# Attention scores in two-bank PSUM tiles, and the products of two groups of heads in one bank

## The chip, the cores and the metric

The kernel runs on one core of a Trainium2 chip. A core has five engines that work in parallel, each through its own instructions in order: TensorE (PE) multiplies matrices, VectorE (DVE) and ScalarE (ACT) work on elements, GpSimd (POOL) and SyncE (SP) do the rest, mostly issuing DMA transfers. PE writes its results to PSUM, which has 2 KB banks on each of 128 partitions: a bank holds 512 float32 values a partition. The metric is the device time of one execution in microseconds (us). Times of the kernel before are the median of three runs, and beside them there is one profiled execution, whose records are read below.

## The reference

One transformer layer over x of shape (8, 512, 128) in float32: eight sequences (B) of 512 tokens (T) with 128 features (D). Causal attention with 16 heads of 8 features comes first, then a mixture of 8 experts of which every token uses its best two. Cut to what matters:

```python
def attn(x):                       # after a layernorm of x
    q = (x @ Wq).reshape(b, t, 16, 8); k, v likewise
    s = einsum('bqhd,bkhd->bhqk', q * 8 ** -0.5, k)
    s = where(causal, s, -inf)
    p = softmax(s)                 # exp(s - max), divided by its sum over keys
    o = einsum('bhqk,bkhd->bqhd', p, v).reshape(b, t, 128)
    return o @ Wo + bo
x = x + attn(layernorm(x))
def moe(x):                        # after a layernorm of x
    probs = softmax(x @ gate_w.T); top2 = top_k(probs, 2)
    out_e = relu(x @ w1[e] + b1[e]) @ w2[e] + b2[e]
    return sum over the token's two experts of prob * out_e
x = x + moe(layernorm(x))
```

## The kernel before

A sequence's 512 tokens are cut into four blocks of 128 (`NT` = 4), and its 16 heads into four groups of four (`G`, `HG`); a group is two pairs of heads. Everything for one pair (sequence b, group g) is done in turn, 32 such groups in all.

**Scores, twice.** `shifts` (lines 555 to 636) computes the scores s = q k^T only to find each row's maximum: PE writes a bank of 512 scores (lines 593 and 598, bf16 operands that hold float32 split into three parts and the causal mask as extra rows), and DVE reduces it to maxima `pm` (line 612). The negated maxima of the group (`nm`, line 618) are turned by PE (line 560), copied by ACT to `nmT` (line 562) and sent by DMA as two more rows of q (line 568). `attend` (lines 638 to 760) then computes the transposed scores st (lines 740 and 745), which now come out with the maximum already subtracted, and ACT takes their exponential into `pt` (line 750), one bank at a time. The products of `pt` with v (line 667) add up in the one PSUM bank `po`: four heads lie in four strips of 32 partitions, of which each uses 9, eight features and a row of sums (v is kept with a column of ones in `va`). After a group's last product ACT copies the bank to `ob` (line 675); `divide` turns it by four PE transposes (`oqp`, line 687), takes the reciprocals of the sums (line 690) and scales (line 691). After the last group of a sequence `out_T` and `out_project` apply Wo.

**Units.** The causal scores of a pair of heads are laid into banks by `S_UNITS` and `T_UNITS` (lines 83 to 92): five banks of 512 columns for each pair and each of the two kinds, as two units of two banks and one unit of a single bank. So a group has ten banks of scores, ten maxima, ten banks of transposed scores and ten exponentials. All these banks come from one pool, `ps_sc`, with four buffers of a bank each (line 123), taken in turn by both kinds; after attention, expert tiles take their hidden layer `ph` (line 1238) from it as well. `ps_mm` has three more banks, and `po` has the eighth.

**Order.** Each engine's order is fixed by the program. Generators such as `project`, `shifts`, `attend`, `route` and `experts` yield virtual times, in units of one sequence, and the one that is due first goes on. `shifts` runs 0.55 ahead of `attend` (`LEAD`), and a unit of scores and a unit of transposed scores come in turn: PE's order is scores, transposed scores, some product, other work, scores again. After each unit of scores one entry of the list `late` is run (maxima turned, then their DMA on SP's queue); after each unit of transposed scores `go_on` runs one waiting product and one waiting step of the output. Layernorms, projections, routing and, from the fourth sequence on, expert tiles lie between these units on every engine.

Of the kernel before, what the change touches and what calls it, by code (L numbers as in the profile page):

```python
# [18 lines left out]
P = 128  # L19
# [7 lines left out]
def preln_attn_moe(ctx: ExitStack, tc: tile.TileContext, x, wq, wk, wv, wo, bo,  # L27
# [54 lines left out]

    S_UNITS = (
        (((0, 3, 0),), ((1, 3, 0),)),
        (((0, 0, 0), (0, 2, P)), ((1, 0, 0), (1, 2, P))),
        (((0, 1, 0), (1, 1, 2 * P)),),
    )
    T_UNITS = (
        (((0, 0, 0),), ((1, 0, 0),)),
        (((0, 1, 0), (0, 3, 3 * P)), ((1, 1, 0), (1, 3, 3 * P))),  # L90
        (((0, 2, 0), (1, 2, 2 * P)),),
    )

# [29 lines left out]
    ps_sc = ctx.enter_context(tc.tile_pool(name="ps_sc", bufs=4, space=PSUM))  # L123
# [106 lines left out]
    def packed_buffers(k):  # L230
        q2 = const.tile([P, H, T], BF16, tag=f"q2{k}", name=f"q2{k}")
        k2 = const.tile([P, H, T], BF16, tag=f"k2{k}", name=f"k2{k}")
        q2_buf.append(q2)
        k2_buf.append(k2)
        va = const.tile([P, NT, H, VC], F32, tag=f"va{k}", name=f"va{k}")
        nc.gpsimd.memset(va[:, :, :, HD:], 1.0)
        va_buf.append(va)
        pm = const.tile([P, HG, 4, 4], F32, tag=f"pm{k}", name=f"pm{k}")
        nc.gpsimd.memset(pm, NEG)
        pm_buf.append(pm)  # L240
        nh = const.tile([P, P], BF16, tag=f"nh{k}", name=f"nh{k}")
        nc.gpsimd.memset(nh, 0.0)
        nh_buf.append(nh)
# [149 lines left out]
    def project():  # L393
# [4 lines left out]
        def arrange(k, groups):  # L398
            for s, w in enumerate((wq_sb, wk_sb)):
                t = const.tile([P, D], F32, tag=f"w{k}{s}", name=f"w_{k}_{s}")  # L400
                nc.scalar.copy(
                    t.rearrange("k (g d h) -> k g d h", g=groups, d=HD),
                    w.rearrange("k (g h d) -> k g d h", g=groups, d=HD),
                )
# [150 lines left out]
    def shifts():  # L555
# [18 lines left out]
        for b in range(B):  # L574
            for g in range(G):
# [5 lines left out]
                pm = pm_buf[g % 2].rearrange("p (n u) t k -> p u n (t k)", u=2)  # L581
                for pr in range(2):
                    n = 2 * g + pr
                    for i, unit in enumerate(S_UNITS):
                        yield t0 + (3 * pr + i) / 24
                        for v, bank in enumerate(unit):
                            ps = ps_sc.tile(
                                [P, T], F32, tag="sc", name=f"s_{b}_{n}_{i}_{v}"
                            )
                            for u, t, at in bank:  # L590
                                h, q = 2 * n + u, ts(t, P)
                                if t > 0:
                                    nc.tensor.matmul(  # L593
                                        ps[:, at : at + t * P], lhsT=q2[:KS, h, q],
                                        rhs=k2[:KS, h, : t * P],
                                        start=(at == 0), stop=True, skip_group_check=True,
                                    )
                                nc.tensor.matmul(  # L598
                                    ps[:, at + t * P : at + (t + 1) * P],
                                    lhsT=q2[:, h, q], rhs=k2[:, h, q],  # L600
                                    start=(at + t == 0), stop=True, skip_group_check=True,
                                )
                            blocks = ps.rearrange("p (a q) -> p a q", q=P)
                            if i == 0:
                                top, src = pm[:, v, pr, 12:13], ps
                            elif i == 1:
                                top, src = pm[:, v, pr, 3:7], blocks
                            else:
                                top, src = pm[:, :, pr, 8], ps.rearrange(
                                    "p (u k) -> p u k", u=2  # L610
                                )
                            nc.vector.tensor_reduce(top, src, AX.X, ALU.max)  # L612
                        if t0 + (3 * pr + i) / 24 < 0:
                            keep_warm(WARM[2], f"{g}_{pr}_{i}")
                        if late:
                            late.pop(0)()
# [21 lines left out]
    def attend():  # L638
# [14 lines left out]
        def at_cols(pt, unit, u, at, W):  # L653
            v = u if len(unit) == 2 else 0
            return pt[:, v, at : at + W]

        def product(b, g, pts, unit, first, last):
            va = va_buf[b % 2]
            for j in sorted({j for bank in unit for _, j, _ in bank}):
                W = T - j * P  # L660
                for pr in range(2):
                    for bank in unit:
                        for u, i, at in bank:
                            if i != j:
                                continue
                            h = 2 * pr + u
                            nc.tensor.matmul(  # L667
                                po[32 * h : 32 * h + VC, j * P :],
                                lhsT=va[:, j, HG * g + h, :],
                                rhs=at_cols(pts[pr], unit, u, at, W),  # L670
                                start=(first and j == 0), stop=(last and j == 2),
                            )
            if last:
# [8 lines left out]
        def divide(b, ob, g):  # L682
            if g == 0:
                on[b] = work.tile([P, NT, D], F32, tag="on", name=f"on_{b}", bufs=1)
            pt = mm_tile(f"oqp_{b}_{g}")
            for t in range(NT):
                nc.tensor.transpose(pt[:, ts(t, P)], ob[:, ts(t, P)], ident)  # L687
            oq = pt.rearrange("p (k r) -> p k r", r=32)
            rd = small.tile([P, NT * HG], F32, tag="rd", name=f"rd_{b}_{g}")
            nc.vector.reciprocal(rd, oq[:, :, HD])  # L690
            nc.vector.tensor_tensor(
                on[b].rearrange("p t (g h d) -> p t g h d", g=G, h=HG)[:, :, g],
                pt.rearrange("p (t h r) -> p t h r", t=NT, h=HG)[:, :, :, 0:HD],
                rd.rearrange("p (t h) -> p t h", t=NT).unsqueeze(3).to_broadcast(
                    [P, NT, HG, HD]
                ),
                ALU.mult,
            )
# [22 lines left out]
        for b in range(B):  # L721
            for g in range(G):
                yield b + g / G
                assert (b, g, 2) in shifted
                q2, k2 = q2_buf[b % 2], k2_buf[b % 2]
                for i, unit in enumerate(T_UNITS):
                    pts = []
                    for pr in range(2):
                        yield b + g / G + (2 * i + pr + 0.5) / 24
                        n = 2 * g + pr  # L730
                        pt = work.tile(
                            [P, 2, T], F32, tag="pt", name=f"pt_{b}_{n}_{i}", bufs=6
                        )
                        for v, bank in enumerate(unit):
                            ps = ps_sc.tile(
                                [P, T], F32, tag="sc", name=f"st_{b}_{n}_{i}_{v}"
                            )
                            for u, j, at in bank:
                                h, k = 2 * n + u, ts(j, P)
# [294 lines left out]
    def experts():  # L1034
# [17 lines left out]
        def after(s, i):  # L1052
            return when(s, quad(s, i)[0]) >= B
# [321 lines left out]
```

## Time and profile before

| | |
|---|---|
| median of three runs | 618.14 us (616.91 to 624.91) |
| the profiled execution | 610.58 us, of which its span 608.9 us |
| mean granted clock of PE | 0.949 |
| PE busy | 526.4 us, 86% |
| DVE busy | 435.1 us, 71% |
| ACT busy | 312.2 us, 51% |
| POOL busy | 188.4 us, 31% |
| maxima of scores (DVE, line 612) | 320, 208 us together, from 25.4 to 448 us |
| exponentials (ACT, line 750) | 320, 177.6 us, from 44.4 to 485 us |
| products with v (PE, line 667) | 1,024, 99.5 us |
| copies of po (ACT, line 675) | 32, 18.9 us |

The span runs from the first to the last instruction of the program. Busy times are those of the instructions' records; a matmul's end is modelled, and matmuls overlap, so a busy PE is not PE at its peak. A row such as "L612 DVE TENSOR_REDUCE pm<-s ... x320 | 206.4, 683 | 31.2" names the line, the engine, the operation and its tiles, the number of instructions, their busy time in us and the mean ns of one, and last the time for which the engine stood idle just before them and what ended that. The chain of work that ended last is followed back from the last instruction: at each step to what released it, or to the instruction before it on its engine.

### The profile page before, as it was taken

The numbers are of one execution on the slowest core, as the hardware profiler recorded it, in microseconds if no ns is written. First come the engines' busy times: TensorE is split into PE (matmuls) and PEld (weight loads), VectorE is DVE, ScalarE is ACT, GpSimd is POOL, SyncE is SP. The second block draws the span as 40 slices with busy tenths as digits, with TensorE's granted clock in tenths as the row PEclk, the third lists the DMA queues.
The fourth block names the chain that finished last, engine by engine and source line by source line (L and its number), as shares of the span: only waits on it lengthen the run. The fifth ranks groups of instructions, "written<-read, shape, count | busy, mean of one in ns | idle before, by whom it ended". The sixth has DMA issues, their size and how long they took to land.

```text
span 608.9 us, 14141 instructions
## 1 busy us (share of the span) xinstructions
PE 526.4 (86%) x4804; PEld 381.0 (63%) x4804; DVE 435.1 (71%) x1407; ACT 312.2 (51%) x685; POOL 188.4 (31%) x220
## 2 busy tenths in 40 slices
PE   7879998988877888889899999998999889889980
PEld 4655455555444554656566677775667579789970
DVE  6787688678986777787888786898684256323594
ACT  2646566655564574546455565564464434244530
POOL 3032200203413230162243213514314534655441
PEclk9989799999987899999899999999899999899995
DMA  2658187286379436521662486232135588667793
GB/s 56 177 135 169 44 215 164 67 186 169 80 152 166 116 96 166 135 60 44 156 145 60 119 173 170 71 87 88 49 81 145 163 252 234 181 196 240 218 315 111
DMA packets 68762, 86.07 MB, mean 141 GB/s; under 512 B 11540, under 2 KB 50748, under 8 KB 66652
## 3 DMA queue, kind: packets, MB, share of 16 engines
q1 hardware_dynamic: 63300, 75.10, 49.0%
q0 software_dynamic: 4800, 9.41, 4.6%
q8 instruction: 39, 0.64, 0.5%
q10 hardware_dynamic: 592, 0.66, 0.3%
q14 instruction: 31, 0.25, 0.2%
HBM read 61.34 MB, written 26.16 MB: 144 GB/s over the span
## 4 chain that ended last, share of the span: by engine, by line
PE 48%; DVE 24%; ACT 9%; DMA 7%; issue 7%; SPq 2%; another core or an unknown queue 1%; POOL 1%; ACTq 0%; DVEq 0%; POOLq 0%
DVE pm L612 11%; PE po L667 10%; PE py L1097 7%; PE ph L1238 6%; ACT pt L750 5%; PE st L745 4%; PE s L593 4%; PE st L740 4%; PE s L598 3%; PE oqp L687 3%; DMA q<-nmT 2%; DMA q<-ys 2%; PE pq L444 2%; DVE x L1316 2%; ACT hT L1245 2%
## 5 line engine op out<-in xcount | busy, mean ns | idle before, releaser
L750 ACT ACTIVATE pt<-st 128x512 f32<-128x512 f32 x320 | 177.6, 599 | 133.3 <-PE st L740 55.5
L612 DVE TENSOR_REDUCE pm<-s 128x1 f32<-128x512 f32 (+2 forms) x320 | 206.4, 683 | 31.2 <-PE s L598 25.7
L1135 POOL DMA_INDIRECT ys<-yo,to x78 | 75.5, 968 | 139.3 <-ACT pt L750 21.6
L593 PE MATMUL s<-k,q 72*128 72x384 bf16 (+2 forms) x384 | 94.6, 282 | 19.5 <-DVE pm L612 9.2
L740 PE MATMUL st<-q,k 128*128 128x128 bf16 x512 | 94.0, 225 | 12.6 <-DMA q<-nmT 4.6
L598 PE MATMUL s<-k,q 128*128 128x128 bf16 x512 | 94.9, 225 | 7.3 <-ACT pt L750 4.9
L667 PE MATMUL po<-pt,va 128*9 128x512 f32 (+3 forms) x1024 | 99.5, 460 | 1.1 <-ACT pt L750 1.0
L1003 POOL DMA_INDIRECT xs<-xn_f,slot x64 | 62.2, 972 | 116.8 <-ACT pt L750 85.1
L745 PE MATMUL st<-q,k 74*128 74x256 bf16 (+2 forms) x384 | 94.6, 284 | 0.0
L1097 PE MATMUL py<-w_sb,hT 128*128 x624 | 87.1, 281 | 7.7 <-issue 4.5
L1097 PEld LDWEIGHTS py<-w_sb,hT 128*128 128x128 f32 x624 | 77.7, 194 | 10.0 <-issue 5.5
L598 PEld LDWEIGHTS <-q 128*128 128x128 bf16 x512 | 51.6, 101 | 30.9 <-issue 27.8
L593 PEld LDWEIGHTS <-q 72*128 72x128 bf16 x384 | 38.2, 101 | 37.7 <-issue 31.3
L740 PEld LDWEIGHTS <-k 128*128 128x128 bf16 x512 | 52.5, 103 | 12.1 <-issue 5.2
L745 PEld LDWEIGHTS <-k 74*128 74x128 bf16 x384 | 38.4, 100 | 19.6 <-issue 14.3
L667 PEld LDWEIGHTS po<-pt,va 128*9 128x9 f32 x1024 | 21.3, 90 | 35.5 <-issue 24.0
L1238 PE MATMUL ph<-xgT,wt 128*128 128x128 f32 x288 | 40.1, 282 | 0.7 <-ACT xgT L1199 0.6
L1238 PEld LDWEIGHTS ph<-xgT,wt 128*128 128x128 f32 x288 | 35.0, 192 | 5.4 <-PE st L740 1.7
L1245 ACT ACTIVATE hT<-ph,q 128x128 f32<-128x128 f32 x72 | 20.9, 371 | 27.9 <-PE ph L1238 14.8
L690 DVE RECIPROCAL rd<-oqp 128x16 f32<-128x16 f32 x32 | 8.2, 255 | 36.9 <-PE oqp L687 31.6
L687 PEld LDWEIGHTS oqp<-ident,ob 128*128 128x128 f32 x128 | 14.4, 148 | 29.7 <-issue 28.3
L454 POOL TENSOR_TENSOR part<-rest,part 128x512 bf16<-128x512 f32 x14 | 16.1, 1158 | 50.0 <-ACT part L453 21.8
(170 smaller groups left out, 717.2 us busy)
## 6 DMA issues: line engine op xcount, KB each, us to landing
wt<-wrows SPq DMA_DIRECT2D x36, 322.0 KB
k<-kparts SPq DMA_DIRECT2D x42, 192.0 KB
q<-wrows SPq DMA_DIRECT2D x24, 322.0 KB
k<-wrows SPq DMA_DIRECT2D x18, 322.0 KB
q<-qparts SPq DMA_DIRECT2D x30, 192.0 KB
q<-ys SPq DMA_DIRECT2D x15, 256.0 KB
k<-xs SPq DMA_DIRECT2D x42, 65.0 KB
qparts<-part SPq DMA_DIRECT2D x14, 192.0 KB
```

Of the source, the lines that this page charges most:

```text
L593: nc.tensor.matmul(ps[:, at : at + t * P], lhsT=q2[:KS, h, q], rhs=k2[:KS, h, : t * P], start=(at == 0), stop=True, skip_group_check=True,)
L598: nc.tensor.matmul(ps[:, at + t * P : at + (t + 1) * P], lhsT=q2[:, h, q], rhs=k2[:, h, q], start=(at + t == 0), stop=True, skip_group_che ...
L612: nc.vector.tensor_reduce(top, src, AX.X, ALU.max)
L667: nc.tensor.matmul(po[32 * h : 32 * h + VC, j * P :], lhsT=va[:, j, HG * g + h, :], rhs=at_cols(pts[pr], unit, u, at, W), start=(first and ...
L740: nc.tensor.matmul(ps[:, at : at + P], lhsT=k2[:, h, k], rhs=q2[:, h, k], start=(at == 0), stop=True, skip_group_check=True,)
L745: nc.tensor.matmul(ps[:, at + P : at + T - j * P], lhsT=k2[:KO, h, k], rhs=q2[:KO, h, (j + 1) * P :], start=False, stop=True, skip_group_c ...
L750: last_exp[0] = nc.scalar.activation(pt[:, v, :], ps, AF.Exp, scale=SCALE)
L1003: ins = nc.gpsimd.indirect_dma_start(out=xs[k], out_offset=bass.IndirectOffsetOnAxis(ap=slot[b][:, j * NT + i : j * NT + i + 1], axis=0), ...
L1097: nc.tensor.matmul(py, lhsT=hT[:, c, :], rhs=w2_sb[:, bass.ds(at[s, i] + c * E * D, D)], start=(c == 0), stop=(c == FC - 1),)
L1135: ins = nc.gpsimd.indirect_dma_start(out=ys[k], out_offset=bass.IndirectOffsetOnAxis(ap=to[s, first][:, i - first : i - first + 1], axis=0 ...
L1238: nc.tensor.matmul(ph[:, ts(c, P)], lhsT=wt[s, i][:, ts(c, P)], rhs=turned[s, first][:, ts(i - first, P)], start=True, stop=True,)
L1245: nc.scalar.activation(hT[:, c, :], ph[:, ts(c, P)], AF.Relu, bias=bias)
```

## The change

It has two parts. First, every unit is two banks, and a tile of `ps_sc` is two banks too, with two buffers instead of four: a group has five units of each kind, each reduced by one maximum instruction or one exponential of 1,024 elements a partition. The single-bank units of a group's two pairs are joined to one. Products are put off to the second, fourth and fifth unit of a group. Second, `va` has 18 columns a head, nine of v and sums and nine of zeros, and the heads are put in another order by the arrangement of Wq's and Wk's columns, so that the products of an even group go to rows 0 to 8 of each strip of `po` and those of the next, odd group to rows 9 to 17 of the same strip: `po` is copied, turned and divided once for two groups. The tiles of the experts' hidden layer take the two halves of a two-bank tile in turn.

```diff
     S_UNITS = (
-        (((0, 3, 0),), ((1, 3, 0),)),
-        (((0, 0, 0), (0, 2, P)), ((1, 0, 0), (1, 2, P))),
-        (((0, 1, 0), (1, 1, 2 * P)),),
+        (((0, 0, 3, 0),), ((0, 1, 3, 0),)),
+        (((0, 0, 0, 0), (0, 0, 2, P)), ((0, 1, 0, 0), (0, 1, 2, P))),
+        (((1, 0, 3, 0),), ((1, 1, 3, 0),)),
+        (((1, 0, 0, 0), (1, 0, 2, P)), ((1, 1, 0, 0), (1, 1, 2, P))),
+        (((0, 0, 1, 0), (0, 1, 1, 2 * P)), ((1, 0, 1, 0), (1, 1, 1, 2 * P))),
     )
...
-    ps_sc = ctx.enter_context(tc.tile_pool(name="ps_sc", bufs=4, space=PSUM))
+    ps_sc = ctx.enter_context(tc.tile_pool(name="ps_sc", bufs=2, space=PSUM))
...
-        va = const.tile([P, NT, H, VC], F32, tag=f"va{k}", name=f"va{k}")
-        nc.gpsimd.memset(va[:, :, :, HD:], 1.0)
+        va = const.tile([P, NT, H, 2 * VC], F32, tag=f"va{k}", name=f"va{k}")
+        nc.gpsimd.memset(va[:, :, :, HD : HD + 1], 1.0)
+        nc.gpsimd.memset(va[:, :, :, VC:], 0.0)
...
-                nc.scalar.copy(
-                    t.rearrange("k (g d h) -> k g d h", g=groups, d=HD),
-                    w.rearrange("k (g h d) -> k g d h", g=groups, d=HD),
-                )
+                for p in range(2):
+                    src = w[:, ts(p, 64)].rearrange("k (h o d) -> k o d h", o=2, d=HD)
+                    of = "k (d o h) -> k o d h" if groups == 2 else "k (o d h) -> k o d h"
+                    nc.scalar.copy(t[:, ts(p, 64)].rearrange(of, o=2, d=HD), src)
...
+                for i, unit in enumerate(S_UNITS):
+                    yield t0 + i / (UNITS * G)
+                    ps = ps_sc.tile([P, 2, T], F32, tag="sc", name=f"s_{b}_{g}_{i}")
+                    for v, bank in enumerate(unit):
+                        for pr, u, t, at in bank:
+                            ...
+                    nc.vector.tensor_reduce(top, src, AX.X, ALU.max)
...
+        def product(b, g, pts, first, last):
+            odd = g % 2
+            va = va_buf[b % 2].rearrange("p c h r -> p c (h r)")
+            ...
+            for j, h, p in sorted(parts, key=lambda a: a[:2]):
+                c0 = 2 * VC * (8 * (g // 2) + 2 * h + odd) - VC * odd
+                nc.tensor.matmul(
+                    po[32 * h : 32 * h + 2 * VC, j * P :], lhsT=va[:, j, c0 : c0 + 2 * VC], rhs=p,
+                    start=(first and j == 0 and not odd), stop=(last and j == 2 and odd == 1),
+                )
-            if last:
+            if last and odd:
                 ob = work.tile([P, T], F32, tag="ob", name=f"ob_{b}_{g}", bufs=1)
                 nc.scalar.copy(ob, po)
...
-            rd = small.tile([P, NT * HG], F32, tag="rd", name=f"rd_{b}_{g}")
-            nc.vector.reciprocal(rd, oq[:, :, HD])
+            rd = small.tile([P, NT * HG, 2], F32, tag="rd", name=f"rd_{b}_{g}")
+            nc.vector.reciprocal(rd, oq[:, :, HD : 2 * VC : VC])
+            for o in range(2):
+                nc.vector.tensor_tensor(
+                    ...
...
+                    pt = work.tile([P, 2, T], F32, tag="pt", name=f"pt_{b}_{g}_{i}", bufs=6)
+                    ps = ps_sc.tile([P, 2, T], F32, tag="sc", name=f"st_{b}_{g}_{i}")
+                    ...
-                            last_exp[0] = nc.scalar.activation(pt[:, v, :], ps, AF.Exp, scale=SCALE)
+                    last_exp[0] = nc.scalar.activation(pt, ps, AF.Exp, scale=SCALE)
+                    pts.append((pt, unit))
+                    go_on()
+                    if i % 2 == 1 or i == UNITS - 1:
+                        products.append(lambda b=b, g=g, pts=pts, i=i: product(
+                            b, g, pts, i == 1, i == UNITS - 1))
+                        pts = []
...
-                ph = ps_sc.tile([P, T], F32, tag="sc", name=f"ph_{s}_{i}")
+                if sum(after(*a) for a in tiles[:n]) % 2 == 0:
+                    two = ps_sc.tile([P, 2, T], F32, tag="sc", name=f"ph_{s}_{i}")
+                    ph = two[:, 0, :]
+                else:
+                    ph = two[:, 1, :]
```

## The prediction

> **What bounds the kernel now.** I read three views first: busy time by stretch, the chain of work that ended last, and the groups of instructions. A stretch of 70 us from the middle, where attention runs beside routing and experts, reads (busy us and instructions by engine, granted clock, DMA share, GB/s):
>
> ```profile
> core 0: us, PE busy (x) PEld busy (x) DVE busy (x) ACT busy (x) POOL busy (x), PEclk, DMA share, GB/s
> 100.00:170.00 70.00, 60.03 (x569) 36.78 (x568) 58.47 (x165) 41.53 (x83) 16.85 (x16) 0.98 0.51 125
> ```
>
> PE and DVE are both busy some 85% and neither all the time: two nearly equal loads, coupled through PSUM, that stop each other. The chain over 25 to 490 us, all of attention (the exponentials start between 44.4 and 484.3 us, so one group of heads takes 440 / 32 = 13.75 us), confirms it:
>
> ```profile
> by line: DVE pm L612 14.0%; PE po L667 13.6%; issue 6.4%; ACT pt L750 6.4%; PE st L745 5.2%; PE s L593 5.2%; PE st L740 4.8%; PE py L1097 4.8%; PE ph L1238 4.7%; PE s L598 3.9%; PE oqp L687 3.4%; DMA q<-nmT 2.8%; PE pq L444 2.4%; PE pl L789
> ```
>
> In us of these 465: the maxima 65.1, the exponentials 29.8, the transposes of the finished output (oqp) 15.8. Each owner gives way to another after a few us. A stretch where DVE owns the chain, the start, length and name of each piece:
>
> ```profile
> 100.72 1.20 DVE pm L612 x2
> 101.91 0.21 DVE stats_f L355
> 102.13 0.02 issue
> 102.15 0.18 DVE mv_f L356
> 102.33 1.17 DVE pm L612 x2
> 103.50 0.26 DVE xn_a L370
> ...
> 109.43 0.22 PE st L740
> ```
>
> DVE goes on for 9 us without a gap, and the next maxima always find their scores ready: while DVE reads the second bank of a pair, PE refills the first. That is what four one-bank buffers buy here. The rest, about 120 us after 490, is experts and DMA and is not touched, but for where the scores of the experts lie.
>
> **Costs of the pieces.** The groups by form (busy, mean ns, idle before):
>
> ```profile
> L750 ACT ACTIVATE pt<-st 128x512 f32<-128x512 f32 x320 | 177.6, 599 | 133.3 <-PE st L740 55.5 <-PE st L745 54.6 <-PE s L598 6.8
> L612 DVE TENSOR_REDUCE pm<-s 128x1 f32<-128x512 f32 x128 | 82.2, 684 | 15.4 <-PE s L598 13.5 <-issue 1.4
> L687 PE MATMUL oqp<-ident,ob 128*128 128x128 f32 x128 | 22.2, 299 | 1.2 <-issue 1.1 <-ACT ob L675 0.2
> L1245 ACT ACTIVATE hT<-ph,q 128x128 f32<-128x128 f32 x72 | 20.9, 371 | 27.9 <-PE ph L1238 14.8 <-PE py L1097 6.8 <-PE xgTp L1197 4.9
> L675 ACT COPY ob<-po 128x512 f32<-128x512 f32 x32 | 18.9, 591 | 3.5 <-PE po L667 1.8 <-PE s L598 1.7
> ```
>
> And the timeline, for a refill of two banks and for how fast PE follows a maximum:
>
> ```profile
> 206.37 0.33 PE L593 MATMUL s<-k,q 72*128 72x384 bf16 x1
> 206.76 0.22 PE L598 MATMUL s<-k,q 128*128 128x128 bf16 x1
> 206.81 0.22 PE L740 MATMUL st<-q,k 128*128 128x128 bf16 x1
> 211.09 0.69 DVE L612 TENSOR_REDUCE pm<-s 128x2 f32<-128x512 f32 x1
> 211.83 0.32 PE L593 MATMUL s<-k,q 72*128 72x384 bf16 x1 [0.68 <-DVE pm L612]
> ```
>
> Two banks are issued in 206.81 - 206.37 = 0.44 us (one bank 0.22) and have ended 0.61 after the start; a refill starts 0.05 after the maximum that frees it.
>
> **Maxima, 320 become 160.** In a stream two take 1.20 (the stretch above), 0.60 each. One of 1,024 elements was never run. Bounds: nothing saved (1.20), or the second costs its elements alone. What an element from PSUM costs DVE is shown by two additions, yo<-py of 128 at 285 ns and x<-pp of 512 at 692: (692 - 285) / 384 = 1.06 ns, so 0.60 + 0.54 = 1.14. I take 1.14, DVE's row being the nearer guide: 0.06 x 160 = 10 us of DVE. On the chain are 65.1 / 1.20 = 54 pairs: 3.2 us.
>
> **Exponentials, 320 become 160.** Two in a stream take 1.08. The rows 371 ns for 128 elements and 599 for 512 give (599 - 371) / 384 = 0.59 ns an element, so 599 + 304 = 903 ns for 1,024; other function and bias, hence the other bound is 1.08, no saving. The skill's ScalarE: Activation LUTs (rules for kernel authors) says about 0.3 us and 0.83 ns an element, which would make one of 1,024 cost 1.15, more than two now; but it gives 0.72 for 512, where the trace has 0.599, so the trace decides. I take the middle, 0.99: 0.09 x 160 = 14 us of ACT, of which 29.8 / 1.08 = 28 pairs lie on the chain: 2.5 us.
>
> **Output, once for two groups.** 64 of 128 transposes go: half of 15.8 on the chain, 7.9 us. 16 copies of 591 ns go, 9.5 us of ACT; on the chain in the share of the exponentials (29.8 of 177.6): 1.6. 16 reciprocals at 255 ns go, 4.1 us of DVE, on the chain in the share of the maxima (65 of 206): 1.3. The scaling multiplications stay 32, the matmuls into po 1,024 with the same columns (18 rows for 9 inside the same 32).
>
> **Sum of the gains on the chain:** 3.2 + 2.5 + 7.9 + 1.6 + 1.3 = 16.5. But PE and DVE are equally loaded: what one gains, the other soon holds. I count half, 8.2.
>
> **The buffers, four of a bank become two of two banks.** Score units and transposed-score units alternate in the program, so each kind is left with one buffer: no refill before the whole of its reader is done, no reader before both banks are full. (a) Inside a stretch of DVE's, the break from reader to reader becomes 0.05 + 0.61 + 0.05 = 0.71, where other DVE work does not fill it. In the fence above it was 0.41, short by 0.30; in the rest of that stretch and in 135 to 142 us the other breaks are 0.92, 1.30, 0.67, 0.80, 0.67, 0.36, 0.48: short 0, 0, 0.04, 0, 0.04, 0.35, 0.23, so 0.12 on average over eight; where two maxima follow with nothing between (38 to 44 us: ten in 6.06) the full 0.71. I take 0.17, near the average of the eight. Of the 54 pairs, some 20 end a stretch: 34 x 0.17 = 5.8. (b) When the chain passes from DVE or ACT back to PE, PE has two banks to fill where one was already full: 0.22. When it passes from PE to DVE, the reader starts a bank later but is 0.06 shorter: 0.16; to ACT 0.22 - 0.09 = 0.13. In the chain's list I count 20 passes from the maxima to PE, 19 from exponentials to PE, 11 from PE to maxima, 19 from PE to exponentials: 39 x 0.22 + 11 x 0.16 + 19 x 0.13 = 12.8. Behind a waiting refill PE's whole queue stands: the other kind's scores, products, expert matmuls. Bounds of (a) and (b): 9 (half is taken up) to 50 (the full 0.71 at all 34, and twice as many passes); nothing excludes the low end, only a gain. Sum taken: 18.6.
>
> A rule speaks against the change here. Perfetto Trace Analysis (optimizing Scalar/DVE operations) grants that larger operations help a saturated engine, and adds: "If Scalar/Vector aren't saturated, but are causing bubbles on other engines, breaking up instructions may allow work to be completed sooner." DVE stands between: 84% busy. By the first half of the rule the kernel would gain up to DVE's 10 + 4 = 14 us, by the second lose the 18.6.
>
> **Small edits, taken at nothing.** Two more ACT copies of half size for each weight pair (now 415 ns at 3.9 and 32.8 us) hide behind layernorm at the start: 0 to +1. Weights of 18 columns for 9 hide under running matmuls (90 ns now; by 148 ns for 128 columns under 5 ns more): 0 to +4. One more memset of 0.2 to 1 us on POOL before the first rows exist. Row-maximum DMAs go out on SP after two of five units for two of six: 13.75 x (2/5 - 2/6) = 0.9 us later; 11 us of distance (0.2 of four groups) covers it, uncovered it adds that in the few places where this DMA is on the chain (13 us in all): 0 to +3, taken as 0; weight fetches of the experts queued behind on SP move as little. Products come in three lumps a group for three before.
>
> **The sum.** The profiled execution took 610.58 us around a span of 608.9. It becomes 610.6 - 8.2 + 18.6 = 621, 10.4 us or 1.7% more. The runs shown have a median of 618.14, 7.6 above it; 618.1 + 10.4 = 629.
>
> **Rivals.** *The fixed costs win* (26%). In each group DVE's work shrinks by (10 + 4) / 32 = 0.44 us and PE's by 11 / 32 = 0.35, of 13.75; if stops do not grow, both floors fall together, and the waits of scores for exponentials (8.3 and 4.9 us), which come from four buffers shared by both kinds, go (by the view of waits): all 16.5 and half of 13, with only 5 of new stops: -18, 600 us. For it: other DVE work fills most breaks. Against: half the breaks seen were too short. *Lockstep* (29%): slower by more. PE now starts a refill before the last maximum of the unit before has ended at 109 of 191 handovers, by 0.76 us on average (matching matmuls and maxima in order), 83 us in all. All of these starts move back; if two fifths reach the end, 33, less 8.2: +25, 643. It decides against no change from a quarter of the 83 on (21 - 8 = 12.4). For it: PE has 10 us in 70 to spare. Against: DVE is busy at most of these times anyway. *It saves nothing per instruction* (part of the same case): the reader's cost runs with its elements; then 5.7 of the 16.5 fall away, 8.2 becomes 5.4, +13.
>
> **How the numbers follow.** My forecast, small growth, 618 to 640, has 45%. A measurement of this kernel tells about 2% from no change, 12.4 us, so to 630.5; a quarter of the forecast's case lies above that. Faster by over 2%: 0.24, the first rival but for its upper end. Same: 0.34 of the forecast and 0.02 of that rival, 0.36. Slower: 0.29 of lockstep and 0.11 of the forecast, 0.40. The range runs from 602, into the first rival, to 648, into lockstep; the likeliest case alone is 618 to 640.
>
> **What would show it.** One maximum of 1,024 at 1.20 to 1.25 us alone, one exponential at 0.90 to 1.08, oqp at half its busy time: else the gains are mis-sized. PE's waits for pm (13.9 us over all lines now) and for pt growing, DVE's breaks between maxima never below 0.7, "PE s" and "PE st" larger in the chain: else (a) and (b) fall. It is wrong if DVE's other work falls into the breaks nearly always, or if a DMA moves: one landing of row maxima alone holds the chain for 8.7 us at 184.6.

## The result, and the profile after

The changed kernel takes 639.75 us where the kernel before takes 619.99: 1.0357 of it (95% interval 1.0303 to 1.0411), 3.6% slower. The prediction, 10.4 us or 1.7% slower, had the direction and about half the size (19.8 us); the time lies in its range. The profiled execution took 634.1 us, its span 632.4, 23.5 more than before: the one before was quick for its kernel, so some 4 us of this are not the change's. The ratios in this document leave out executions that are over 1.5% slower than the fastest of their kernel.

The span can be cut where the last exponential ends, the end of attention. That was at 484.9 us and is at 494.9: attention lost 10.0 us. The rest, experts and sums, took 123.9 us and takes 137.5: 13.6 more, in a part that the prediction had called untouched. Each stage is one execution, and the experiments below correct the two shares.

The chain of work that ended last can't be followed back through attention in this profile. So the view by stretch and the groups by form answer for it, first the 70 us shown of before (busy us and instructions by engine, granted clock, DMA share, GB/s):

```profile
core 0: us, PE busy (x) PEld busy (x) DVE busy (x) ACT busy (x) POOL busy (x), PEclk, DMA share, GB/s
100.00:170.00 70.00, 55.81 (x539) 34.59 (x539) 53.31 (x137) 35.02 (x46) 16.83 (x16) 0.93 0.52 130
```

PE fell from 60.0 to 55.8 us of 70 and DVE from 58.5 to 53.3: both stand more. The groups (busy, mean ns of one, idle before and what ended it):

```profile
L745 ACT ACTIVATE pt<-st 128x1024 f32<-128x1024 f32 x160 | 163.9, 1025 | 146.2 <-PE st L740 80.1 <-PE st L735 51.1 <-issue 3.7
L615 DVE TENSOR_REDUCE pm<-s 128x2 f32<-128x1024 f32 x64 | 78.1, 1220 | 27.0 <-PE s L603 25.7 <-PE xnTp_f L392 0.6 <-PE py L1094 0.3
L683 PE MATMUL oqp<-ident,ob 128*128 128x128 f32 x64 | 10.9, 295 | 1.8 <-ACT ob L671 1.8
L671 ACT COPY ob<-po 128x512 f32<-128x512 f32 x16 | 9.3, 583 | 0.4 <-PE po L665 0.4
```

A maximum of 1,024 elements takes 1.22 us alone and an exponential 1.025, near what was forecast; transposes and copies of the output are halved. The savings are all there as busy time, and the kernel is slower. The view of waits tells where it stands (engine and line, what it waited for, us in total, times, longest):

```profile
DVE pm L615 <- PE s L603: 68.7, 66, 9.1
ACT hT L1246 <- PE ph L1239: 42.0, 28, 2.9
PE ph L1239 <- DVE hT L1248: 15.4, 15, 3.4
PE s L598 <- ACT pt L745: 15.1, 15, 1.7
PE s L603 <- DVE pm L615: 13.4, 16, 1.9
PE s L598 <- DVE pm L615: 12.6, 17, 2.2
```

and of before:

```profile
DVE pm L612 <- PE s L598: 25.7, 33, 2.2
PE s L593 <- DVE pm L612: 9.2, 12, 2.0
PE s L593 <- ACT pt L750: 8.3, 14, 2.3
```

DVE's waits for scores were 25.7 us and are 68.7. PE's waits for maxima grew from 13.9 to 29.3 (with 3.3 of the transposed scores), and those of scores and transposed scores for exponentials from 16.3 to 27.0: PE stands 56.3 us for these readers, where it stood 30.2. And there is a wait that no row of before had: a hidden layer, ph, that waits for DVE's part of the one before, 15.4 us.

The timeline of attention shows the new rhythm (start, duration, engine, line, operation, the wait before):

```profile
107.13 1.22 DVE L615 TENSOR_REDUCE pm<-s 128x8 f32<-128x1024 f32 x1
108.26 0.28 DVE L363 BATCH_NORM_STATS2 stats_f<-x 128x6 f32<-128x128 f32 x1
108.40 0.32 PE L598 MATMUL s<-k,q 72*128 72x384 bf16 x1 [1.18 <-DVE pm L615]
...
109.33 0.31 DVE L378 TENSOR_SCALAR xn_a<-x,mv_a,rstd_a 128x128 f32<-128x128 f32 x1
109.54 1.02 ACT L745 ACTIVATE pt<-st 128x1024 f32<-128x1024 f32 x1 [1.77 <-PE st L740]
109.56 1.22 DVE L615 TENSOR_REDUCE pm<-s 128x2 f32<-128x1024 f32 x1
...
110.83 0.22 PE L603 MATMUL s<-k,q 128*128 128x128 bf16 x1 [1.38 <-DVE pm L615]
```

PE stands 1.2 to 1.4 us before both refills, until the whole maximum is done. DVE's break is filled with layernorm work. So the price is paid here on PE, and through it by ACT, which waits 1.77 us for its scores behind the refill.

The tail, hidden layers (ph), their relu on ACT and DVE (hT) and second products (py), in the kernel after:

```profile
567.23 1.06 PE L1239 MATMUL ph<-xgT,k 128*128 128x128 f32 x8
...
569.29 0.35 DVE L1248 TENSOR_SCALAR hT<-ph,k 128x128 f32<-128x128 f32 x1 [1.29 <-issue]
569.70 1.16 PE L1239 MATMUL ph<-xgT,k 128*128 128x128 f32 x8 [0.19 <-DVE hT L1248]
570.69 1.06 PE L1094 MATMUL py<-w_sb,hT 128*128 x8
...
571.59 1.06 PE L1239 MATMUL ph<-xgT,q 128*128 128x128 f32 x8
```

and before:

```profile
555.28 1.06 PE L1238 MATMUL ph<-xgT,q 128*128 128x128 f32 x8
555.91 1.66 ACT L1245 ACTIVATE hT<-ph,q 128x128 f32<-128x128 f32 x6 [1.49 <-PE py L1097]
556.82 0.35 DVE L1247 TENSOR_SCALAR hT<-ph,q 128x128 f32<-128x128 f32 x1 [0.72 <-PE ph L1238]
557.07 1.06 PE L1238 MATMUL ph<-xgT,q 128*128 128x128 f32 x8
```

Before, the next hidden layer starts 1.79 us after the last one, while the relu of the last is still running. After, the one at 569.70 starts 0.06 us after the relu of the one before has ended, and the next, at 571.59, waits for no relu. This fits a second half of a two-bank tile that is written only when the readers of the first half are done, though it is another bank; the first experiment tests it. Two hidden layers then take 2.47 + 1.89 us.

### The profile page after: what moved, and what is told of

Read it like the earlier page. It is cut to its first block, busy times and chain, and to the rows that moved or that the text cites. A ratio compares the mean times of both kernels' runs of the same rounds, so it can differ in the third digit from the quotient of the medians.

```text
span 632.4 us, 13591 instructions
## 1 busy us (share of the span) xinstructions
PE 513.6 (81%) x4736; PEld 375.6 (59%) x4736; DVE 425.2 (67%) x1231; ACT 294.6 (47%) x513; POOL 188.6 (30%) x222
## 5 line engine op out<-in xcount | busy, mean ns | idle before, releaser
L615 DVE TENSOR_REDUCE pm<-s 128x8 f32<-128x1024 f32 (+2 forms) x160 | 194.8, 1220 | 71.4 <-PE s L603 68.7
L745 ACT ACTIVATE pt<-st 128x1024 f32<-128x1024 f32 x160 | 163.9, 1025 | 146.2 <-PE st L740 80.1
L598 PE MATMUL s<-k,q 72*128 72x256 bf16 (+2 forms) x384 | 88.9, 282 | 31.2 <-ACT pt L745 15.1
L603 PE MATMUL s<-k,q 128*128 128x128 bf16 x512 | 89.1, 225 | 19.6 <-DVE pm L615 13.4
L735 PE MATMUL st<-q,k 128*128 128x128 bf16 x512 | 87.7, 223 | 18.9 <-DMA q<-nmT 9.1
L665 PE MATMUL po<-pt,va 128*18 128x512 f32 (+3 forms) x1024 | 95.5, 463 | 0.0
L740 PE MATMUL st<-q,k 74*128 74x256 bf16 (+2 forms) x384 | 88.4, 280 | 0.0
L665 PEld LDWEIGHTS po<-pt,va 128*18 128x18 f32 x1024 | 21.4, 98 | 31.4 <-issue 26.6
L1239 PE MATMUL ph<-xgT,q 128*128 128x128 f32 x192 | 27.7, 289 | 10.1 <-DVE hT L1248 9.7
L1239 PEld LDWEIGHTS ph<-xgT,q 128*128 128x128 f32 x192 | 24.1, 197 | 13.1 <-DVE hT L1248 11.4
```

The source lines that it names most:

```text
L598: nc.tensor.matmul(ps[:, v, at : at + t * P], lhsT=q2[:KS, h, q], rhs=k2[:KS, h, : t * P], start=(at == 0), stop=True, skip_group_check=True,)
L603: nc.tensor.matmul(ps[:, v, at + t * P : at + (t + 1) * P], lhsT=q2[:, h, q], rhs=k2[:, h, q], start=(at + t == 0), stop=True, skip_group_ ...
L665: nc.tensor.matmul(po[32 * h : 32 * h + 2 * VC, j * P :], lhsT=va[:, j, c0 : c0 + 2 * VC], rhs=p, start=(first and j == 0 and not odd), st ...
L735: nc.tensor.matmul(ps[:, v, at : at + P], lhsT=k2[:, h, k], rhs=q2[:, h, k], start=(at == 0), stop=True, skip_group_check=True,)
L740: nc.tensor.matmul(ps[:, v, at + P : at + T - j * P], lhsT=k2[:KO, h, k], rhs=q2[:KO, h, (j + 1) * P :], start=False, stop=True, skip_grou ...
L745: last_exp[0] = nc.scalar.activation(pt, ps, AF.Exp, scale=SCALE)
```

## The experiments

Each is compared with the kernel before on its own chip; two chips differ by some 20 us in the time of the same kernel, so ratios are what is compared. In the order below, these runs shared a chip: the first of the tail and the three on merging; the two repeats; the two short readers and the two halves of the change; the three on divided, fewer and more banks; the sixth pass and the first with seven banks; the next two with seven banks. The last was alone on its chip. The same kernel, run on two chips, has differed by 0.8 and 1.0 points in its ratio, so a difference of about 1% between two chips shows nothing by itself. "Nothing merged" is: each bank a tile of its own with its own reader.

**The tail's wait taken away.**

```diff
-                if sum(after(*a) for a in tiles[:n]) % 2 == 0:
-                    two = ps_sc.tile([P, 2, T], F32, tag="sc", name=f"ph_{s}_{i}")
-                    ph = two[:, 0, :]
-                else:
-                    ph = two[:, 1, :]
+                ph = ps_sc.tile([P, 2, T], F32, tag="sc", name=f"ph_{s}_{i}")[:, 0, :]
```

> The changed kernel, but each hidden layer of an expert has a two-bank tile for itself (one bank of it unused), so no matmul writes into a tile of which another engine still reads the other half. Theory: of the 23.5 us by which the span grew, some 10 come from attention and some 13 from the experts' tail, where the second half of a tile waited for the reader of the first; with that wait gone the time is 1.010 to 1.018 of before, and from the last exponential to the end it takes 124 us as before, not 137. Rival: the tail is bound by weights and rows that come by DMA, the new wait only stands where another stood; then the ratio stays at 1.030 or above.

Measured: 1.019 (1.0101 to 1.0278), and once more, beside another run:

> The changed kernel with a two-bank tile for each hidden layer once more, on one chip with the next run, for what merging is worth in all. Theory: two-bank hand-over costs some 2.5% and the merged instructions give back 1.6%: 1.012 to 1.024 of before, 0.5 to 1.5% slower than nothing merged. Rival: merging is neutral, the two runs agree within 0.4%.

Measured: 1.0265 (1.0214 to 1.0317). PE's wait for DVE before ph is 5.9 us in the second of these, in 3 places, for 15.4 in 15. The change itself stands at 1.0357, so the halves of a tile cost 0.9 to 1.7%, 6 to 10 us: a little less than the theory had. From the last exponential to the end it takes 130.4 and 130.8 us, where the change takes 137.5 and the theory had 124. So the wait is worth about 7 us there; why the rest stays above the 123.9 of before was not tested. What is left of the ratio, 1.9 to 2.7% or 12 to 16 us, is put down to attention.

The chain of the second of these runs can be followed. Over 25 to 490 us, as in the prediction:

```profile
by line: PE po L665 14.2%; DVE pm L615 10.7%; PE s L598 6.7%; PE st L740 6.6%; issue 6.3%; PE ph L1235 5.5%; PE st L735 5.4%; ACT pt L745 5.3%; PE s L603 4.9%; PE py L1094 4.7%; DMA q<-qparts 2.7%; DMA q<-nmT 2.6%; PE pq L453 2.3%; PE oqp L
```

The maxima fall from 14.0% to 10.7 and the exponentials from 6.4 to 5.3; the four rows of scores and transposed scores on PE rise from 19.1% to 23.6, which is 21 us.

**Which merging costs.** Scores and transposed scores get a pool each: two one-bank buffers, or one of two banks.

```diff
-    ps_sc = ctx.enter_context(tc.tile_pool(name="ps_sc", bufs=2, space=PSUM))
+    ps_s = ctx.enter_context(tc.tile_pool(name="ps_s", bufs=2, space=PSUM))
+    ps_t = ctx.enter_context(tc.tile_pool(name="ps_t", bufs=2, space=PSUM))
...
-                    ps = ps_sc.tile([P, 2, T], F32, tag="sc", name=f"s_{b}_{g}_{i}")
                     for v, bank in enumerate(unit):
+                        ps = ps_s.tile([P, T], F32, tag="sc", name=f"s_{b}_{g}_{i}_{v}")
...
+                        nc.vector.tensor_reduce(top, src, AX.X, ALU.max)
```

> The changed kernel with nothing merged: units of two banks in the order of the change, but each bank a tile of its own with its own maximum or exponential of 512 elements, two buffers for scores and two for transposed scores, four in turn for the experts' hidden layers; the output for two groups stays as changed. Theory (merged buffers cost the attention time): this is faster than before by what the output part saves, 8 us of the 16 less transposes' worth, 0.985 (0.978 to 0.995). Rival (the loss of the attention stage comes from the new order of products, heads and units): it stays slower than before, 1.01 to 1.02.

Measured: 1.0101 (0.9989 to 1.0214), and once more:

> New units and the output for two groups, nothing merged, once more, beside the run before this one. Theory (the output part saves nothing by itself, but new units alone gave 1.0205): 1.008 to 1.020. Rival (the output part gains where attention has become slower): below 1.008.

Measured: 1.0203 (1.015 to 1.0257).

> As the run with nothing merged, but the scores for the maxima are in one two-bank tile with one maximum of 1,024 elements; the exponentials stay one for each bank, with two buffers. Theory: DVE must wait for PE to refill both banks after every maximum; 160 of these breaks, at 0.1 us left after other work, make it slower than nothing merged by 10 to 20 us, 1.005 to 1.015 of before. Rival (the exponentials' tile is what PE stands on, since PE waits for ACT first after a unit): as fast as nothing merged within 4 us.

Measured: 1.0371 (1.028 to 1.0462).

> As the run with nothing merged, but the transposed scores are in one two-bank tile with one exponential of 1,024 elements; the maxima stay one for each bank. Theory: ACT has slack, so its breaks are covered, and the time is within 6 us of nothing merged, 0.985 to 0.995 of before. Rival (the exponentials' tile is what PE stands on): slower than nothing merged by 10 us and more, 1.00 to 1.015.

Measured: 1.0185 (1.0046 to 1.0323).

My theory failed at the first of these: with nothing merged the kernel was forecast faster than before and is 1 to 2% slower. A loss of about the size of attention's is there with nothing merged. Merging both adds 0.6 to 0.9% (1.0265 against 1.0203 on one chip, 1.019 against 1.0101 on the other), within the intervals; and in the profiles of the first pair attention ends at 502.1 and 501.7 us, so nearly all of the 3.8 us between their spans lies behind it. Beside nothing merged, the other two came out as their theories had it: merged maxima 17 us slower, merged exponentials 5. Merged maxima alone were slower than both merged: PE waits 62.8 us for maxima there, where it waits 28.3 for maxima and 28.0 for exponentials with both merged. That run also had the lowest granted clock on this chip, 0.914 for 0.943 of before; why, I did not find out.

These runs do not differ in merging alone. With a pool for each kind no score waits for an exponential; in the change, where both kinds share a pool, scores do so at 24 of their 57 waits for readers. So the pools apart are not the division that the change has, and what merging costs by itself is not shown. The two runs with one kind merged also give the hidden layers three tiles in turn for four.

**What a merged instruction is worth.** The two-bank tiles of the first experiment, read by two instructions of 512 elements each:

```diff
-                    nc.vector.tensor_reduce(top, src, AX.X, ALU.max)
+                    for v, bank in enumerate(unit):
+                        ...
+                        nc.vector.tensor_reduce(top, src, AX.X, ALU.max)
...
-                    last_exp[0] = nc.scalar.activation(pt, ps, AF.Exp, scale=SCALE)
+                    for v in range(2):
+                        last_exp[0] = nc.scalar.activation(
+                            pt[:, v, :], ps[:, v, :], AF.Exp, scale=SCALE
+                        )
```

> The changed kernel with a tile of its own for each hidden layer, and with every two-bank tile read by two maxima or exponentials of 512 elements: the readers begin when both banks are full and free both at once, as in the change, but no instruction is longer than before. Theory (the hand-over by two banks costs, the longer instruction itself saves): slower than the merged one by 3 to 8 us, 1.022 to 1.033 of before. Rival (an instruction of 1,024 elements costs more than its time, by holding its engine): faster than the merged one, 1.005 to 1.015.

Measured: 1.0354 (1.0245 to 1.0464), from two executions. Beside the runs with nothing merged (1.010 and 1.020, and, on the same chip, the new units alone below without the output part, 1.0205) handing over by two banks costs 1.5 to 2.5%; beside the merged ones (1.019 and 1.0265) the longer instructions give 0.9 to 1.6% back. Both go the way that the theory had. The intervals overlap and most of these pairs are of two chips, so neither size is shown.

**Each half of the change alone.** The output for two groups in the kernel before (its diff is that of `va`, `arrange`, `product` and `divide` in the change), and the new units without it and with nothing merged:

> The kernel before with the second part of the change alone: v with 18 columns a head, heads in the new order, the bank of products copied, turned and divided once for two groups; units, buffers, maxima and exponentials as before. Theory of the prediction: half of 16.5 less the readers' share, about 5 to 8 us less, 0.988 to 0.995. Rival (what the output took was time in which PE stood by anyway, or kept its clock up): within 0.3% of before.

Measured: 0.9994 (0.9951 to 1.0037).

> The kernel before with the new units alone: five units of two banks for a group in place of six, products in lumps after the second, fourth and fifth unit, two one-bank buffers for each kind in place of four shared; every bank still has its own maximum or exponential, and the output is taken group by group as before. Nothing is merged. Theory: the order of units costs nothing, 0.995 to 1.005; together with the output part alone it gives the 1.010 of the run that had both. Rival: the separate pairs of buffers and the lumps cost the attention stage on their own, 1.01 to 1.02, and the output part gains what was forecast.

Measured: 1.0205 (1.0139 to 1.0271). The rival held in the first run: the output part is worth nothing there, at most 0.5% by its interval. In the second the units cost 2% by themselves.

**Why the units cost: room.** The kernel before with its four score banks divided in two pairs; with three of them; with five, for which the other matmuls give one up:

```diff
-    ps_sc = ctx.enter_context(tc.tile_pool(name="ps_sc", bufs=4, space=PSUM))
+    ps_s = ctx.enter_context(tc.tile_pool(name="ps_s", bufs=2, space=PSUM))
+    ps_t = ctx.enter_context(tc.tile_pool(name="ps_t", bufs=2, space=PSUM))
```

> The kernel before with its own units, but its four score banks divided: two for the scores, two for the transposed scores, as the strict turn of two-bank units divides them in the change; the experts' hidden layers take the two pairs in turn. Nothing else is changed. Theory (the four shared banks with units of one bank between give PE room to run ahead, and that is what the new units lose): 1.012 to 1.022, as the run with the new units alone. Rival (the new units lose by five steps a group instead of six, through which fewer steps of output, products and row maxima pass): 0.997 to 1.005.

Measured: 1.0102 (1.0067 to 1.0136).

> The kernel before with three one-bank buffers for all scores and hidden layers in place of four. Theory (room between PE and its readers is what sets attention's time): one bank less costs 1.02 to 1.05. Rival (the stops come from DVE's and PE's work, not from buffers): within 1% of before.

Measured: 1.0761 (1.0667 to 1.0854).

> The kernel before with five one-bank buffers for scores and two for all other matmuls, in place of four and three. Theory: more room for the scores saves 0.5 to 1.5%, if the two other buffers do not cost it: 0.985 to 1.00. Rival: 1.00 to 1.02, since projections, transposes and experts now wait for a bank.

Measured: 1.0333 (1.0274 to 1.0392).

One score bank less costs 7.6% (from two executions), more than forecast. A fifth one that is taken from the other three costs 3.3%, more than either side forecast, though PE's waits for the readers of scores fall to 16.6 us: the other matmuls are short of banks too. Dividing the four costs 1.0%, between the theory and its rival, and half of what the new units cost, whose run has its pools apart too. Before, a unit of one bank shifts the turn, and each kind can find its next bank earlier than the strict pairs give it. The waits of the divided pairs, in the view of waits, then of the new units alone:

```profile
PE s L594 <- DVE pm L613: 18.4, 30, 1.4
PE s L599 <- DVE pm L613: 15.3, 40, 1.5
PE s L598 <- DVE pm L615: 22.8, 51, 1.4
PE s L603 <- DVE pm L615: 14.2, 29, 2.5
```

33.7 us of PE's waiting for maxima with the divided pairs, where the kernel before has 11.0 at these two lines; with the waits for exponentials, which fell, PE stands 40.0 us for 30.2. The new units have 37.0 at these lines and 38.7 in all, no more than the divided pairs: the other half of their cost doesn't show in these waits. Was it the five passes a group for six?

```diff
                     pts.append((pt, unit))
                     go_on()
+                    if i == UNITS - 1:
+                        go_on()
```

> The new units with nothing merged and the output group by group, but at the last unit of a group two waiting steps of each list are taken instead of one, so that six pass in a group as before. Theory (units of two banks leave less room): no better than without it, 1.016 to 1.026. Rival (five passes instead of six hold back products and row maxima): back to what the divided banks alone cost, 1.007 to 1.013.

Measured: 1.0292 (1.0232 to 1.0352). No: a sixth pass makes it no better. A rival was not tested: the granted clock. On its chip the run with the new units alone had a mean of 0.936 for 0.947 of before, while the divided pairs had theirs almost as before, 0.948 for 0.949. Executions of one kernel differ in this way too: of the kernel before on one chip, one at 0.940 took 597.5 us and one at 0.957 took 590.8, 1.1% more time for 1.8% less clock. By this estimate some 0.7 of the units' 2.0% go with the clock. Whether the lower clock is a cause here or comes of the standing, no run shows.

The last experiments gave room: all seven banks in one pool.

```diff
-    ps_sc = ctx.enter_context(tc.tile_pool(name="ps_sc", bufs=4, space=PSUM))
-    ps_mm = ctx.enter_context(tc.tile_pool(name="ps_mm", bufs=3, space=PSUM))
+    ps_sc = ctx.enter_context(tc.tile_pool(name="ps_sc", bufs=7, space=PSUM))
...
-        return ps_mm.tile([P, T], F32, tag="mm", name=name)
+        return ps_sc.tile([P, T], F32, tag="sc", name=name)
```

> The kernel before, with its seven banks for scores, hidden layers and all other matmuls in one pool, taken in turn, in place of four and three. Theory (room is what is short): scores often find more than four banks, and it is faster than before, 0.985 to 0.997. Rival (a bank that a projection or an expert holds for long stops all that comes after it in the turn): 1.00 to 1.02.

Measured: 0.982 (0.9768 to 0.9872).

> The new units with nothing merged and the output group by group, with all seven banks for scores and other matmuls in one pool in turn. Theory (the units of two banks lack room): the distance to the kernel before with the same pool (0.982) shrinks from 2% to under 1%, so 0.980 to 0.992 of before. Rival (the order of the units and of what stands between them costs): it stays, 0.997 to 1.008.

Measured: 0.9773 (0.9718 to 0.9827).

> The kernel before with the output taken once for two groups and one pool of seven banks. Theory (the output's time lies beside other work): as the pool alone, 0.977 to 0.987. Rival (what the output part saves was hidden by the stops for banks): 0.965 to 0.976.

Measured: 0.9616 (0.9551 to 0.9682).

> New units and the output for two groups, nothing merged, with one pool of seven banks. Theory (with room the units cost nothing): as the output part alone with that pool, 0.955 to 0.967. Rival (units of two banks still cost where the output is taken together): 0.972 to 0.985.

Measured: 0.9743 (0.9669 to 0.9816).

The new units, 2% slower than the old ones with four banks, are level with them with seven (0.9773 against 0.982, on two chips): room cures the loss. And the output part, worth nothing with four banks, saves 2% with seven (0.9616 against 0.982). The intervals are apart, but the chips are two, so its size is uncertain by about 1%. Together with the new units it saves nothing clear (0.9743 against 0.9773), so the old units stay ahead by 1.3 to 1.6%, as the rival of the last run had it; of the two differences the 1.6 is of one chip (0.9616 against 0.9773). The best kernel is the one before with the output for two groups and one pool of seven banks: 3.8% faster than before. Its stretch of 70 us:

```profile
100.00:170.00 70.00, 66.06 (x623) 39.66 (x620) 62.41 (x178) 42.12 (x85) 19.34 (x18) 0.98 0.52 131
```

PE is at 66.1 us for 60.0, DVE at 62.4 for 58.5: less standing on both. PE's waits of scores and transposed scores for their readers are 2.4 us in all, where the kernel before has 30.2; the two largest rows:

```profile
PE s L593 <- DVE pm L612: 0.8, 4, 0.2
PE st L748 <- ACT pt L758: 0.7, 2, 0.4
```

## Why the prediction was wrong in size

The step that failed most is the tail, which the prediction put at nothing: it cost 6 to 10 us, and the forecast of 10.4 fell 9.4 short of the measured 19.8. Attention lost 12 to 16 us by the runs without the tail's wait, close to the 10.4; but that was in part luck, since the output part was given a gain that it did not have, and the longer instructions too small a one.

**The costs of the buffers, 18.6 us.** The size was somewhat low: the divided pairs (1.0%), the rest of the units' loss (1.0%) and the two-bank hand-over (1.5 to 2.5%) add up to 3.5 to 4.5%, 22 to 28 us, by runs that do not divide the banks as the change does, and of which the merged instructions give a part back. That too little room between PE and its readers costs time was right. Of the two steps, (b), 12.8 us, fits: it put the price on PE, which has two banks to fill when the chain comes back to it, and in the chain shown under the first experiment PE's scores have 21 us more. Step (a), 5.8 us, put it into DVE's breaks, of at least 0.71 us. Of 159 breaks between maxima in the profile after, 36 are shorter and the mean is 1.51, long enough for a refill; the timeline shows PE standing instead. And the costs were to begin at merging, while 1.0 to 2.0% are lost with nothing merged and a pool for each kind: that the shared turn of four banks is worth something, as the divided pairs show, was not seen. Nor is each kind left with one buffer of its own in the change, as the step has it: scores wait for exponentials there too.

**The gains, 16.5 us, counted at half, 8.2.** The terms were sized well: a maximum at 1.22 us alone for the expected 1.20 to 1.25, an exponential at 1.025 for 0.90 to 1.08, half the transposes. But the half was right for neither part. The longer instructions gave some 0.9 to 1.6%, 6 to 10 us, where 5.7 stood on the chain. The output part, with 10.8 of the 16.5 (transposes, copies, reciprocals), gave 0.0% by itself. In the chain of that run its transposes do fall, from 3.4% to 2.0, and the DMA of row maxima (q<-nmT) rises from 2.8% to 4.3; PE's waits for the readers of scores are no longer than before, about 25 us for 30. So what took the saving up stays open. With seven banks the part gives 2%, about 12 us, as much as the chain had promised.

**The tail, taken as not touched.** This failed outright and makes up the largest part of the miss: 6 to 10 us by the runs without the wait, about 7 in their profiles. The 13.6 of the first two profiles hold more than this wait. The prediction named the place ("where the scores of the experts lie") and looked at the number of buffers, still four banks, not at what a matmul into one half of a tile has to wait for.

**The small edits** at nothing can't be told apart from nothing: the output part, which holds most of them, measures 0.9994 (0.9951 to 1.0037).

**The rivals.** That fixed costs win is excluded: the whole is 3.6% slower. Lockstep was forecast at +25 us, and 19.8 was measured; but attention alone, for which it was told, lost 12 to 16. The rule of the Trainium skill's Perfetto Trace Analysis (optimizing Scalar/DVE operations) that was weighed, breaking instructions up where they cause bubbles on others, has a counterpart in the hand-over here, which costs where it is coarser (1.0354 against 1.0205 on one chip); and the half that speaks for larger instructions agrees with the two-bank tiles, which were better with one long reader (1.019, 1.0265) than with two short ones (1.0354), on other chips. The rule of 0.3 us and 0.83 ns an element in ScalarE: Activation LUTs (rules for kernel authors) would give 1.15 us for the exponential of 1,024, measured at 1.025. But its slope was right: (1025 - 599) / 512 = 0.83 ns an element, with 0.17 us fixed. The rule gives its 0.3 us for a bias passed as a pointer, and the exponential's call has no bias. The relu rows, from which the prediction took 0.59 ns, have one; set beside each other, the two mix a difference of the fixed part into the slope. The prediction set the rule aside altogether where only its fixed part was for another case.

Still open are the last 1.0% of the new units with four banks, which the room of seven cures, but for which no single wait was isolated and the clock was not excluded; and why merged maxima alone made PE wait longer for maxima than both merged did for both. One rival is untested for all of attention: in the chains of the divided pairs and of the new units the two DMAs that fill q (q<-nmT and q<-qparts) have 47 and 45 us of 25 to 490, where the kernel before has 13. But the faster kernels with seven banks have 27 to 59, so these shares do not follow the time.

## What to carry to other kernels

When a chain passes to and fro between PE and the readers of its PSUM tiles, first ask how many banks each kind can hold at once and in what pieces they come free; fewer, longer instructions on two-bank tiles take that room away, and a saving elsewhere on the chain may show only once there is room, as the output part did with the old units. Pools that are each short can be better joined than enlarged at each other's cost: here seven banks in one turn gave 1.8%, five and two lost 3.3%. When a tile is made larger, look for every other user of its pool: a second half that waits for the first half's readers turns a pipeline into steps. And when a chain is read from one profile, count what the change does behind it as well.

## What was not expected of the hardware and its program

Three score banks for four cost 7.6%, 45 us in 596. The output part was worth 0.0% with four and three banks and 2% with seven in one pool. The mean granted clock was lower in many slower kernels: 0.914 with merged maxima alone for 0.943 of before on one chip, with three banks 0.929 for 0.949. But it isn't so in all: with five score banks it was 0.947 for 0.949, at 3.3% more time.
